# Seven block products in place of eight in layer 0, and sums begun in PSUM by ACT, in a four-layer graph kernel

## Chip, core and metric

One NeuronCore of a Trainium2 chip runs the whole kernel. The metric is device time in microseconds, as the median of several runs. Everything is float32.

The engines named below are PE (matrix products, results in PSUM), ACT and DVE (elementwise work, both read and write PSUM), POOL (elementwise work on SBUF alone) and SP, which issues all the DMAs here. PSUM has eight banks of 128 x 512 float32; a bank is one tile `ps`.

## What is computed

The input `x` is 64 graphs x 256 nodes x 128 features; one 256 x 256 adjacency matrix `adj` serves all. Four layers follow one another, each of the form x = layernorm(x + f(x)):

```python
def step(h, _):                                   # layer 0: five of these steps
    m_in = jnp.einsum('nm,bmd->bnd', in_matrix, h)
    m_out = jnp.einsum('nm,bmd->bnd', out_matrix, h)   # both matrices are adj
    av = jnp.concatenate([m_in, m_out], axis=-1)
    u3 = h @ u3_w.T + u3_b
    z = jax.nn.sigmoid(av @ w3_w.T + w3_b + u3)
    r = jax.nn.sigmoid(av @ w4_w.T + w4_b + u3)
    hv = jnp.tanh(av @ w5_w.T + w5_b + (r * h @ u5_w.T + u5_b))
    h = (1.0 - z) * h + z * hv
...
# layer 1: A = softmax of edge values; M = identity
out = einsum('ij,bjg->big', A * M, x @ W[0]) + einsum('ij,bjg->big', A * (1 - M), x @ W[1]) + bias
# layer 2: attention over adj (softmax of leaky scores, times adj), layernorm, relu -> h_gat
h_gin = (1.0 + eps) * h_gat + einsum('mn,bnh->bmh', A_final, h_gat)
z = relu(layernorm(h_gin @ W1 + b1));  f = relu(z @ W2 + b2 + h_gat)
# layer 3: x, adj x, adj^2 x, adj^3 x, each times a weight, for two copies of adj; their sum
```

## The kernel before

**Tiling.** Two graphs make a pair; there are 32 pairs. A pair's state is one 128 x 512 tile: four blocks of 128 nodes x 128 features (graph b, node half j, block 2b + j). What a layer needs the other way round (features on partitions) is the state turned.

**Message product.** `spread(i, right)` (L499) computes the product with a 256 x 256 matrix, and leaves it turned in one PSUM bank: for each graph b the two node halves are the stationary operands and two rows of blocks of `right`, 256 columns wide, are streamed. That is four products of 256 columns, or eight block products of 128 x 128 x 128. A float32 product is two matmul instructions, each with a weight load of its own. `to_sbuf` (L463) and `evacuate` (L208) copy the bank to SBUF, by ACT or DVE. `spread` is called five times in layer 0 with `aT`, once in layer 1 (`offT`), once in layer 2 (`ginT`) and once in layer 3 (`aT`).

**Layer 0** (L592) runs five steps. Each is a spread, five products of 512 columns (L599, L600, L607, L614, L615), three Tanh by ACT (L603, L609, L617), four elementwise operations of DVE (L605, L619, L620, L622), and a turn of the new state.

**Turning** (`turn`, L471) goes by DMA for most pairs: DVE transposes 32 x 32 blocks (L486), one DMA stores the tile to DRAM (L488), four more load it back (L494). For the last `BY_DMA[site]` pairs of a site PE transposes instead (L480), and ACT or DVE copies the result out.

**The other layers.** `products` (L630) multiplies the four blocks by one or two 128 x 128 weights, 128 columns at a time (L636). Its result in PSUM gets a bias or a residual added by DVE on the way out: L652 in layer 1, L718 and L725 in layer 2. `scale_stats` (L547) takes the mean square by ACT or DVE, POOL raises it to the power -1/2 (L571), and `scale_tokens` (L574) multiplies by it, on ACT, DVE or POOL. Layer 1's diagonal part turns x1 and multiplies the turned tile by `drow` (L645), a row that PE makes from the diagonal at the start (L389). Layer 3 (L730) has the products with `vx`, `vq` (L743, L744) and with the square of adj (L751).

**Order.** Nothing is issued as it is written. Every operation goes to a `Schedule` (L82) with the engines it may run on, a duration for each, and what it reads and writes. `order` (L111) plans the program before it is built: at each turn it takes, of all operations whose inputs are planned, the one that can start first (for operations with several possible engines, the one that ends first), ties by a due time (`DUE` per pair, `LAST_DUE` for the last `LAST` pairs, `HOLD` per layer). `MARGIN` stretches the durations of all engines but PE, `LAG` and `SEEN` are added before another engine sees a result. `PORT` (L40) keeps a POOL operation and a `DVE+` operation (two inputs from SBUF) apart in the plan. Tiles come from the counts in `CLASSES` (L36): 34 working tiles `A`, 15 states `X`, 8 banks `PS`. Each engine then runs its own list strictly in the planned order, each instruction waiting on semaphores for what it needs.

Of the kernel before, what the change touches and what calls it, by code (L numbers as in the profile page):

```python
# [17 lines left out]
BY_DMA = {"h": 1, "y": 1, "x1": 2, "x2": 1, "w": 0, "z": 1, "x3": 1}  # L18

WARM = 4  # L20

# [19 lines left out]


DUE, LAST_DUE, LAST = 15.0, 7.0, 6

MARGIN, LAG = 1.1, 0.3

HOLD = (0.0, 0.0, 0.0, 110.0)
# [7 lines left out]
class Value:  # L55
# [6 lines left out]

    def at(self, *shape):

        n = 1
        for s in shape:
            n *= s
        t = self.ap[:, :n]
        if len(shape) < 2:
            return t  # L70
        names = "abcd"[:len(shape)]
        return t.rearrange(f"p ({' '.join(names)}) -> p {' '.join(names)}", **dict(zip(names[1:], shape[1:])))

# [8 lines left out]
class Schedule:  # L82
# [6 lines left out]
    def add(self, ways, r=(), w=(), dma=None):  # L89

        op = Op(self.pair, ways, list(r), list(w), len(self.ops), dma)
        for v in op.reads:
            op.before.update(dict.fromkeys(v.writers))
        for v in op.writes:
            op.before.update(dict.fromkeys(v.readers))
        for v in op.reads:
            v.readers.append(op)
        for v in op.writes:  # L100
            v.writers.append(op)
        op.before.pop(op, None)
        op.layer = self.layer
        self.ops.append(op)
        return op
# [5 lines left out]
    def order(self, tiles):  # L111
        for op in self.ops:
            op.waits = len(op.before)
            for b in op.before:
                b.then.append(op)
            for v in dict.fromkeys([*op.reads, *op.writes]):
                v.left += 1
        for op in reversed(self.ops):
            us = min(w[1] for w in op.ways) + op.seen
            op.rest = us + max((x.rest for x in op.then if x.pair == op.pair), default=0.0)  # L120
        free = {cls: [(0.0, t) for t in ts] for cls, ts in tiles.items()}
        engines = dict.fromkeys([*SEEN, "PORT"], 0.0)
        ready = [op for op in self.ops if not op.waits]
        out, moved = [], 0.0
        while ready:
            best = None
            for op in ready:
                held = 0.0
                for v in op.writes:
                    if v.cls and v.ap is None:  # L130
                        held = max(held, min((t for t, _ in free[v.cls]), default=1e9))
                if held == 1e9:
                    continue
                for engine, us, fn in op.ways:
                    us = us if engine == "PE" else us * MARGIN
                    start = max(op.ready, held, *(engines[e] for e in USES.get(engine, (engine,))))
                    late = self.due(op.pair) - op.rest + HOLD[op.layer] if op.pair >= 0 else -1e4
                    key = (start + (us if len(op.ways) > 1 else 0.0), late, op.number)
                    if best is None or key < best[0]:
                        best = key, start, op, engine, us, fn  # L140
            if best is None:
                raise RuntimeError("no operation can start: too few tiles")
            _, start, op, engine, us, fn = best
            ready.remove(op)
            for v in op.writes:
                if v.cls and v.ap is None:
                    slot = min(free[v.cls], key=lambda s: s[0])
                    free[v.cls].remove(slot)
                    v.ap = slot[1]
            end = start + us  # L150
            engines.update(dict.fromkeys(USES.get(engine, (engine,)), end))
            if op.dma:
                wait, move, seen = op.dma
                moved = max(moved, end + wait) + move * MARGIN
                op.seen = moved + seen - end + LAG
            out.append((start, op.number, op, fn))
            for v in dict.fromkeys([*op.reads, *op.writes]):
                v.left -= 1
                v.end = max(v.end, end + op.seen)
                if not v.left and v.cls:  # L160
                    free[v.cls].append((v.end, v.ap))
            for x in op.then:
                x.waits -= 1
                same = engine != "SP" and x.ways[0][0].rstrip("+") == engine.rstrip("+")
                x.ready = max(x.ready, end + (0.0 if same else op.seen))
                if not x.waits:
                    ready.append(x)

            for v in dict.fromkeys([*op.reads, *op.writes]):
                op.__dict__.setdefault("tiles", {})[v] = v.ap  # L170
        assert len(out) == len(self.ops), "operations that wait for one another"
        self.span = max(engines.values())
        return [(op, fn) for _, _, op, fn in sorted(out, key=lambda x: x[:2])]
# [3 lines left out]
def kernel(ctx: ExitStack, tc: tile.TileContext, x, xT, adj, adjT, mats, cols, rows, out):  # L177
# [206 lines left out]

    drow, offT = fixed([N], "drow"), fixed([2, N], "offT")

    def diagonal():
        for it in range(2):
            nc.tensor.matmul(t4.at(2, P)[:, it, :], ones.ap[:, :P], dg.ap[:, it, :], start=True, stop=True)  # L389
    pe(mm(256), diagonal, [ones, dg], [t4])  # L390
    dve(0.4, lambda: nc.vector.tensor_copy(drow.ap, t4.at(N)), [t4], [drow])
# [53 lines left out]

    centre(vx, lambda: vx.ap, 2)
    centre(vq, lambda: vq.ap, 2)


# [49 lines left out]
    def spread(i, right):  # L499

        t = Value("PS", name="ps")
        for b in range(2):
            def fn(b=b):
                for j in range(2):
                    nc.tensor.matmul(t.at(2, N)[:, b, :], tokens(i)[:, 2 * b + j, :], right.ap[:, j, :],  # L505
                                     start=(j == 0), stop=(j == 1))
            pe(mm(512), fn, [i, right], [t])
        return t

# [82 lines left out]
    def layer0(x0, hT):  # L592
        h = x0
        for s in range(STEPS):
            mT = to_sbuf(spread(h, aT), "mT")
            t = Value("PS", name="ps")
# [14 lines left out]
            t = Value("PS", name="ps")  # L611
# [18 lines left out]
    def products(lefts, rights, name="ps"):  # L630

        t = Value("PS", name=name)
        for c in range(4):
            def fn(c=c):
                for k, (i, w) in enumerate(zip(lefts, rights)):
                    nc.tensor.matmul(tokens(t)[:, c, :], tokens(i)[:, c, :], w(), start=(k == 0), stop=(k == len(lefts) - 1))  # L636
            pe(mm(128 * len(lefts)), fn, [*lefts, W1], [t])
        return t

    def layer1(x1):  # L640
        qT = to_sbuf(spread(x1, offT), "qT")
        xb, dd = Value("A", name="xb"), lambda: drow.ap[:, None, :].to_broadcast([P, 2, N])
        if by_dma("x1"):
            dT = turn(x1, "dT", "x1")
            dve_or_pool(lambda e: e.tensor_mul(dT.at(2, N), dT.at(2, N), dd()), [drow, dT], [dT])  # L645
        else:
            t, dT = transposes(x1), Value("A", name="dT")
            dve(TT, lambda: nc.vector.tensor_mul(dT.at(2, N), t.at(2, N), dd()), [t, drow], [dT])
        dve_or_pool(lambda e: e.tensor_add(tokens(xb), tokens(x1), row("l1_bias", 4)), [x1, rbc], [xb])
        o = products([qT, dT], [lambda: mat("l1w1"), lambda: mat("l1w0")])  # L650
        y = Value("A", name="y")
        dve(TT, lambda: nc.vector.tensor_add(tokens(y), tokens(o), tokens(xb)), [o, xb], [y])  # L652
        scale_norm(y, x1)

    def layer2(x2):
# [20 lines left out]
        nm, nm2, den, d2 = (lambda k=k: s.at(32)[:, 4 * k:4 * k + 4] for k in range(4))  # L676
# [6 lines left out]
        def largest():  # L683
            nc.vector.tensor_add(nm(), nm(), hs()[:, :, D])
            nc.vector.tensor_scalar(nm2(), nm(), -1.0, None, op0=ALU.mult)
            nc.vector.scalar_tensor_tensor(nm(), nm(), -0.2, nm2(), op0=ALU.mult, op1=ALU.min)
        dve2(0.5, largest, [s, h], [s])
# [12 lines left out]
        t = Value("PS", name="ps")  # L700
        for b in range(2):
            def fn(b=b, t=t):
                for it in range(2):
                    for jt in range(2):
                        nc.tensor.matmul(tokens(t)[:, 2 * b + it, :], wT.at(8, P)[:, 4 * b + 2 * it + jt, :],  # L705
                                         hs()[:, 2 * b + jt, :D], start=(jt == 0), stop=(jt == 1))
            pe(mm(512), fn, [wT, h], [t])
# [8 lines left out]
        t = products([gT], [lambda: mat("w1")])  # L716
        z = Value("A", name="z")
        dve(TT, lambda t=t: nc.vector.tensor_add(tokens(z), tokens(t), row("b1", 4)), [t, rbc], [z])  # L718
        scale_norm(z, z)
# [3 lines left out]
        t = products([zT], [lambda: mat("w2")])  # L723
        y = Value("A", name="y")
        dve(TT, lambda t=t: nc.vector.tensor_add(tokens(y), tokens(t), tokens(hb)), [t, hb], [y])  # L725
        dve2(TT, lambda: nc.vector.scalar_tensor_tensor(y.at(512), y.at(512), 0.0, x2.at(512), op0=ALU.max, op1=ALU.add),
            [y, x2], [y])
        layer_norm(y, x2)

    def layer3(x3, p):  # L730
# [5 lines left out]
        for i in range(2):  # L736
            t = Value("PS", name="ps")
# [80 lines left out]
```

## Time and profile before

| | |
|---|---|
| median of 7 runs | 1520.1 us (1519.96 to 1520.8) |
| the profiled execution's own time | 1520.64 us |
| its span, first to last instruction | 1518.9 us |
| granted PE clock | 0.999 |
| DMA, mean busy share of 16 engines | 69.3% (queue q1), 215.34 MB |

The span is what the profile divides. The page gives busy times by engine, the same in 40 slices, the DMA queues, the chain of work that ended last, and groups of instructions by line of the code. A busy PE is a modelled figure, since its instructions overlap: an instruction of 512 columns is shown as 592 ns, while the next starts some 430 ns later. Prices of products are therefore taken from the distance between starts, which is what the chain gives. A DVE instruction too is shown with a tail that the next one overlaps.

Waits that the trace names most (us in total): ACT L603 on PE L600, 162.0; ACT L617 on PE L615, 160.6; ACT L210 on PE L505, 126.7; DVE L605 on ACT L603, 76.9; DVE L619 on ACT L617, 65.9. PE is in the list only with 0.33 us on a DMA, and with "issue" gaps of its weight loads, which lie under products that run.

### The profile page before, as it was taken

What the parts mean: (1) busy time and instruction counts of PE and PEld (TensorE: products, weight loads), DVE (VectorE), ACT (ScalarE), POOL (GpSimd) and SP (SyncE); (2) the same over time, 40 slices, a digit from 0 to 9 for tenths busy, and PEclk for the clock granted to TensorE, in tenths of its full rate; (3) what the DMA queues carried; (4) which work ended last, traced back from release to release, by engine and by line L of the source; (5) the groups of instructions that cost most, each with busy time, mean ns of one, the idle gap of its engine ahead of it and who ended that gap; (6) DMA issues with size and microseconds to landing.
All of it is one profiled execution on the core that took longest, in us unless ns stands there. A gap on an engine that the chain in (4) does not pass through costs nothing.

```text
span 1518.9 us, 22720 instructions
## 1 busy us (share of the span) xinstructions
PE 1511.0 (99%) x6300; PEld 1052.4 (69%) x6300; DVE 1184.0 (78%) x2774; ACT 901.4 (59%) x2497; POOL 362.7 (24%) x461
## 2 busy tenths in 40 slices
PE   9999999999999999999999999999999999999998
PEld 6555566666666766777677767666776676779987
DVE  6567878888898879888878778778787877887763
ACT  3444445566667767767656665656565556676752
POOL 0000001122323413332222303112331122224542
PEclk9999999999999999999999999999999999999999
DMA  8354557677688697877968777748677767575562
GB/s 237 73 111 97 118 115 149 140 145 161 146 173 158 150 187 149 175 150 170 171 130 174 153 153 160 160 98 164 140 148 152 147 133 144 103 144 118 119 131 64
DMA packets 949454, 216.79 MB, mean 143 GB/s; under 512 B 728144, under 2 KB 944848, under 8 KB 949328
## 3 DMA queue, kind: packets, MB, share of 16 engines
q1 hardware_dynamic: 949328, 215.34, 69.3%
q8 instruction: 51, 0.84, 0.2%
q14 instruction: 75, 0.61, 0.1%
HBM read 117.12 MB, written 98.11 MB: 142 GB/s over the span
## 4 chain that ended last, share of the span: by engine, by line
PE 99%; DMA 1%; SPq 0%; issue 0%; DVE 0%; POOLq 0%; ACT 0%; ACTq 0%; POOL 0%; DVEq 0%
PE ps L505 29%; PE ps L614 9%; PE ps L615 9%; PE ps L607 9%; PE ps L599 9%; PE ps L600 9%; PE ps L636 8%; PE ps L705 4%; PE ps L751 4%; PE ps L743 4%; PE ps L744 4%; PE ps L664 2%; DMA x<-x_in 0%; SPq L494 0%; PE ps L270 0%; PE ps L480 0%
## 5 line engine op out<-in xcount | busy, mean ns | idle before, releaser
L210 ACT COPY a<-ps 128x512 f32<-128x512 f32 (+1 forms) x295 | 160.3, 545 | 187.3 <-PE ps L505 126.7
L505 PE MATMUL ps<-aT,a 128*128 128x256 f32 x1024 | 242.7, 379 | 0.3 <-DMA a<-e 0.3
L505 PEld LDWEIGHTS ps<-aT,a 128*128 128x128 f32 x1024 | 193.4, 190 | 69.1 <-issue 45.4
L603 ACT ACTIVATE a<-ps,bzrh 128x512 f32<-128x512 f32 x160 | 109.9, 687 | 167.4 <-PE ps L600 162.0
L617 ACT ACTIVATE a<-ps,bzrh 128x512 f32<-128x512 f32 x160 | 109.8, 687 | 164.1 <-PE ps L615 160.6
L614 PE MATMUL ps<-a,w 128*128 128x512 f32 x320 | 163.5, 592 | 0.0
L600 PE MATMUL ps<-a,w 128*128 128x512 f32 x320 | 163.4, 592 | 0.0
L615 PE MATMUL ps<-a,u5h 128*128 128x512 f32 x320 | 163.4, 592 | 0.0
L607 PE MATMUL ps<-a,w 128*128 128x512 f32 x320 | 162.9, 592 | 0.0
L636 PEld LDWEIGHTS ps<-W,a 128*128 128x128 f32 x1024 | 128.9, 192 | 21.6 <-issue 18.9
L486 DVE STREAM_TRANSPOSE a<-a 128x512 f32<-128x512 f32 x186 | 131.0, 706 | 11.4 <-ACT a L582 4.2
L571 POOL TENSOR_TENSOR s<-s,neg_half 128x4 f32<-128x4 f32 x128 | 137.1, 1072 | 10.1
L605 DVE SCALAR_TENSOR_TENSOR a<-a,a 128x512 f32<-128x512 f32 x128 | 88.6, 692 | 63.0 <-ACT a L603 60.1
L609 ACT ACTIVATE a<-ps,bzrh 128x512 f32<-128x512 f32 x160 | 109.8, 686 | 45.6 <-PE ps L607 43.7
L619 DVE TENSOR_TENSOR a<-a,a 128x512 f32<-128x512 f32 x128 | 90.0, 703 | 54.8 <-ACT a L617 54.6
L636 PE MATMUL ps<-W,a 128*128 128x128 f32 x1024 | 131.3, 275 | 0.0
L599 PE MATMUL ps<-a,W 128*128 128x512 f32 x256 | 130.8, 593 | 0.0
L524 POOL TENSOR_SCALAR s<-s 128x4 f32<-128x4 f32 x64 | 21.4, 334 | 453.3 <-DVE s L521 444.6
L620 DVE SCALAR_TENSOR_TENSOR a<-a,a 128x512 f32<-128x512 f32 x160 | 117.3, 733 | 12.2 <-ACT a L609 7.1
L568 POOL TENSOR_SCALAR s<-s 128x4 f32<-128x4 f32 x96 | 29.0, 302 | 392.6 <-ACT a L563 304.8
L505 PE MATMUL ps<-aT,x 128*128 128x256 f32 x512 | 122.3, 382 | 0.1
L600 PEld LDWEIGHTS ps<-a,w 128*128 128x128 f32 x320 | 60.8, 190 | 76.5 <-issue 72.5
(181 smaller groups left out, 2731.5 us busy)
## 6 DMA issues: line engine op xcount, KB each, us to landing
e<-a SPq DMA_DIRECT2D x278, 256.0 KB
a<-e SPq DMA_DIRECT2D x1112, 64.0 KB
e<-b SPq DMA_DIRECT2D x32, 512.0 KB
b<-e SPq DMA_DIRECT2D x128, 128.0 KB
x<-x_in SPq DMA_DIRECT2D x32, 256.0 KB
t<-xT_in SPq DMA_DIRECT2D x32, 256.0 KB
a<-d SPq DMA_DIRECT2D x32, 256.0 KB
y_out<-a SPq DMA_DIRECT2D x32, 256.0 KB
```

Of the source, the lines that this page charges most:

```text
L210: S.add([("ACT", us[0], lambda: nc.scalar.copy(o(), i())), ("DVE", us[1], lambda: nc.vector.tensor_copy(o(), i()))], r, w)
L486: dve(n / 512 * 0.55 + 0.09, lambda: nc.vector.transpose(st.at(n), i.at(n)), [i], [st])
L505: nc.tensor.matmul(t.at(2, N)[:, b, :], tokens(i)[:, 2 * b + j, :], right.ap[:, j, :], start=(j == 0), stop=(j == 1))
L571: pool(1.02, lambda: nc.gpsimd.tensor_tensor(rs(), rs(), neg_half.ap, op=ALU.pow), [s, neg_half], [s])
L599: nc.tensor.matmul(t.at(512), mat("u3"), hT.at(512), start=True, stop=False)
L600: nc.tensor.matmul(t.at(512), w4.ap, mT.at(512), start=False, stop=True)
L603: act(0.59, lambda t=t, r=r: nc.scalar.activation(r.at(512), t.at(512), AF.Tanh, bias=bzrh.ap[:, 1:2], scale=0.5), [t, bzrh], [r])
L607: pe(mm(512), lambda t=t, mT=mT: nc.tensor.matmul(t.at(512), w3.ap, mT.at(512), start=False, stop=True, skip_group_check=True), [w3, mT, t ...
L614: nc.tensor.matmul(t.at(512), w5.ap, mT.at(512), start=True, stop=False)
L615: nc.tensor.matmul(t.at(512), u5h.ap, r.at(512), start=False, stop=True)
L620: dve2(TT, lambda hv=hv, z=z: nc.vector.scalar_tensor_tensor(hv.at(512), z.at(512), 1.0, hv.at(512), op0=ALU.add, op1=ALU.mult), [hv, z], ...
L636: nc.tensor.matmul(tokens(t)[:, c, :], tokens(i)[:, c, :], w(), start=(k == 0), stop=(k == len(lefts) - 1))
```

## The change

**Layer 0's message product.** A new `spread7` takes the place of `spread` and its copy, in all five steps (`FAST`) of pairs 0 to 28 (`FIRST`, `FINAL`). It treats the four blocks of the state as a 2 x 2 block matrix (graph by node half) and multiplies it by the 2 x 2 blocks of `aT` with seven block products (Winograd's form of Strassen's scheme). Four sums of state blocks are formed first, by DVE or POOL; four sums of blocks of `aT` (`aTt`) are made once at the start. The products go to the four quarters of one bank, some of them added to what an earlier product left there; between them DVE adds and ACT or DVE copies read single quarters of the same bank.

**Sums begun in PSUM.** `seed` copies a residual or a bias from SBUF into a bank (ACT, or DVE), and `products` adds to it, so the separate DVE additions L652, L718 and L725 go. `scale_norm` then reads the bank itself, and so does the last sum of layer 2 (L726). The planner gives a seed only a bank whose last value was written by products over its whole width.

**Smaller parts.** Layer 1 scales x1 by the diagonal as a column before the turn, in place of after it; `drow` and its products (L389) go. Three small DVE operations for the softmax become two (L684 to L686). `BY_DMA` changes: layer 0's last pair now turns by DMA, and one more pair each at `y`, `x1`, `x2`, `x3` and three at `w` turn on PE. The planner's constants change, and a dependent operation on the same engine is now planned 0.12 us later (`AGAIN`).

```diff
-BY_DMA = {"h": 1, "y": 1, "x1": 2, "x2": 1, "w": 0, "z": 1, "x3": 1}
+BY_DMA = {"h": 0, "y": 2, "x1": 3, "x2": 2, "w": 3, "z": 1, "x3": 2}
+FAST = (0, 1, 2, 3, 4)
+FIRST, FINAL = 0, 3
+AGAIN = {"DVE": 0.12, "POOL": 0.12}
+SPARE = {"DVE": 0.0, "DVE+": 0.0, "POOL": 0.0}
-DUE, LAST_DUE, LAST = 15.0, 7.0, 6
-MARGIN, LAG = 1.1, 0.3
-HOLD = (0.0, 0.0, 0.0, 110.0)
+DUE, LAST_DUE, LAST = 20.0, 9.0, 8
+MARGIN, LAG = 1.03, 0.8
+HOLD = (0.0, -20.0, 0.0, 80.0)
...
-                        held = max(held, min((t for t, _ in free[v.cls]), default=1e9))
+                        held = max(held, min((t for t, a in free[v.cls] if full.get(id(a)) or not v.seeded), default=1e9))
...
-                x.ready = max(x.ready, end + (0.0 if same else op.seen))
+                x.ready = max(x.ready, end + (AGAIN.get(engine.rstrip("+"), 0.0) if same else op.seen))
...
-    def diagonal():
-        for it in range(2):
-            nc.tensor.matmul(t4.at(2, P)[:, it, :], ones.ap[:, :P], dg.ap[:, it, :], start=True, stop=True)
-    pe(mm(256), diagonal, [ones, dg], [t4])
-    dve(0.4, lambda: nc.vector.tensor_copy(drow.ap, t4.at(N)), [t4], [drow])
+    dcol, offT = fixed([2], "dcol"), fixed([2, N], "offT")
+    dve(0.3, lambda: nc.vector.tensor_reduce(dcol.ap, dg.ap, AX.X, ALU.add), [dg], [dcol])
...
+    aTt = fixed([4, P], "aTt")
+    blk_a = lambda j, i: aT.ap[:, j, i * P:(i + 1) * P]
+    for k, (p_, q_) in enumerate(((lambda: blk_a(0, 1), lambda: blk_a(0, 0)), (lambda: blk_a(1, 1), lambda: aTt.ap[:, 0, :]),
+                                  (lambda: blk_a(1, 1), lambda: blk_a(0, 1)), (lambda: blk_a(1, 0), lambda: aTt.ap[:, 1, :]))):
+        dve(0.25, lambda k=k, p_=p_, q_=q_: nc.vector.tensor_sub(aTt.ap[:, k, :], p_(), q_()), [aT, aTt], [aTt])
...
+    def seed(us, o, i, r):
+        t = Value("PS", name="ps")
+        t.seeded = True
+        evacuate(lambda: o(t), i, r, [t], us)
+        return t
...
+    def spread7(h, right, terms):
+        sv, t, o = Value("A", name="sums"), bank(), Value("A", name="mT")
+        p1, p2, p3, p4 = (Part(sv) for _ in range(4))
+        X, Y, Z, V = (Part(t) for _ in range(4))
+        o1, o2, o3 = (Part(o) for _ in range(3))
+        blk = lambda v, k, n=1: v.at(512)[:, k * P:(k + n) * P]
+        H = lambda b, j: lambda: blk(h, 2 * b + j)
+        B = lambda j, i: lambda: right.ap[:, j, i * P:(i + 1) * P]
+        T = lambda k: lambda: terms.ap[:, k, :]
+        s1, s2, s3, s4 = (lambda k=k: blk(sv, k) for k in range(4))
+        def add(o, x, y, op, r, w):
+            fn = lambda e: e.tensor_tensor(o(), x(), y(), op=op)
+            S.add([("DVE+", 0.2, lambda: fn(nc.vector)), ("POOL", 0.42, lambda: fn(nc.gpsimd))], r, w)
+        def product(k, left, rt, r, w, start=False):
+            pe(mm(128), lambda: nc.tensor.matmul(blk(t, k), left(), rt(), start=start, stop=True, skip_group_check=True),
+               [*r, right, terms], w)
+        def plus(to, k, other, r, w, n=1):
+            dve(0.065 + 0.135 * n, lambda: nc.vector.tensor_add(to(), t.at(4, P)[:, k:k + n, :], other()), r, w)
+        def copy(to, k, r, w):
+            S.add([("ACT", 0.18, lambda: nc.scalar.copy(to(), blk(t, k))),
+                   ("DVE", 0.2, lambda: nc.vector.tensor_copy(to(), blk(t, k)))], r, w)
+        product(0, H(0, 0), B(0, 0), [h], [X, Y, Z, V], start=True)
+        copy(lambda: blk(o, 3), 0, [X], [o3])
+        add(s1, H(1, 0), H(1, 1), ALU.add, [h], [p1])
+        add(s2, s1, H(0, 0), ALU.subtract, [h, p1], [p2])
+        add(s3, H(0, 0), H(1, 0), ALU.subtract, [h], [p3])
+        add(s4, H(0, 1), s2, ALU.subtract, [h, p2], [p4])
+        product(0, H(0, 1), B(1, 0), [h, X], [X])
+        copy(lambda: blk(o, 0), 0, [X], [o])
+        product(1, s2, T(1), [p2, Y], [Y])
+        plus(lambda: blk(sv, 1), 1, lambda: blk(o, 3), [Y, o3], [p2])
+        product(2, s1, T(0), [p1, V], [V])
+        product(3, s3, T(2), [p3, Z], [Z])
+        plus(lambda: blk(sv, 0), 2, lambda: blk(sv, 1), [V, p2], [p1])
+        product(2, s4, B(1, 1), [p4, V], [V])
+        plus(lambda: blk(o, 3), 3, lambda: blk(sv, 0), [Z, p1, o3], [o])
+        product(3, H(1, 1), T(3), [h, Z], [Z])
+        plus(lambda: o.at(4, P)[:, 1:3, :], 2, lambda: blk(sv, 1)[:, None, :].to_broadcast([P, 2, P]), [V, Z, p2], [o], 2)
+        return o
...
-            mT = to_sbuf(spread(h, aT), "mT")
+            mT = spread7(h, aT, aTt) if s in FAST and FIRST <= S.pair < n_pairs - FINAL else to_sbuf(spread(h, aT), "mT")
...
-        o = products([qT, dT], [lambda: mat("l1w1"), lambda: mat("l1w0")])
-        y = Value("A", name="y")
-        dve(TT, lambda: nc.vector.tensor_add(tokens(y), tokens(o), tokens(xb)), [o, xb], [y])
-        scale_norm(y, x1)
+        t = seed((0.49, 0.61), tokens, lambda: tokens(xb), [xb, qT, dT])
+        scale_norm(products([qT, dT], [lambda: mat("l1w1"), lambda: mat("l1w0")], t), x1)
...
-        t = products([gT], [lambda: mat("w1")])
-        z = Value("A", name="z")
-        dve(TT, lambda t=t: nc.vector.tensor_add(tokens(z), tokens(t), row("b1", 4)), [t, rbc], [z])
-        scale_norm(z, z)
+        t, z = seed((0.49, 0.61), tokens, lambda: row("b1", 4), [rbc, gT]), Value("A", name="z")
+        scale_norm(products([gT], [lambda: mat("w1")], t), z)
...
-        t = products([zT], [lambda: mat("w2")])
-        y = Value("A", name="y")
-        dve(TT, lambda t=t: nc.vector.tensor_add(tokens(y), tokens(t), tokens(hb)), [t, hb], [y])
-        dve2(TT, lambda: nc.vector.scalar_tensor_tensor(y.at(512), y.at(512), 0.0, x2.at(512), op0=ALU.max, op1=ALU.add),
-            [y, x2], [y])
+        t, y = seed((0.49, 0.61), tokens, lambda: tokens(hb), [hb, zT]), Value("A", name="y")
+        products([zT], [lambda: mat("w2")], t)
+        dve(TT, lambda t=t: nc.vector.scalar_tensor_tensor(y.at(512), t.at(512), 0.0, x2.at(512), op0=ALU.max, op1=ALU.add),
+            [t, x2], [y])
```

## The prediction

> **What bounds the kernel now.** I read the page's busy times first, then the chain of waits, then the chain in order of time for the price of each product, then stages of the run for the slack of the other engines.
>
> ```profile
> PE 1511.0 (99%) x6300; PEld 1052.4 (69%) x6300; DVE 1184.0 (78%) x2774; ACT 901.4 (59%) x2497; POOL 362.7 (24%) x461
> PE 99%; DMA 1%; SPq 0%; issue 0%; DVE 0%; POOLq 0%; ACT 0%; ACTq 0%; POOL 0%; DVEq 0%
> ```
>
> The busy share alone would prove little, but the chain that ended last is PE too: each product is released by the product before it, not by DVE, ACT or a transfer. PE runs from 1.20 to 1512.6 us nearly without a gap, then 6.3 us of statistics and the store remain. So a product's price is on the path, and all other work is free while it arrives in time.
>
> ```profile
> 20.07 0.22 PE ps L314 x2
> 43.01 3.45 PE ps L505 x16
> 46.47 0.86 PE ps L599 x2
> 502.00 3.57 PE ps L636 x32
> 1471.94 0.44 PE ps L480 x4
> ```
>
> Columns: start, us, what, instructions. Two instructions make one product. L505 gives 3.45/8 = 0.431 us for 256 columns, so a whole spread is 1.725. L599 gives 0.86 for 512. L636 gives 3.57/16 = 0.223 for 128 columns, 3.5% dearer per column. L314 streams a single column and still takes 0.22: that is the price of the two weight loads, so 128 columns are where the load and the stream meet. Four transposes on PE cost 0.44.
>
> ```profile
> 400.00:600.00 200.00, 199.67 (x840) 134.97 (x839) 173.89 (x386) 140.54 (x400) 63.58 (x70) 1.00 0.83 164
> 1450.00:1480.00 30.00, 30.00 (x162) 27.00 (x161) 18.09 (x59) 15.92 (x63) 11.77 (x19) 1.00 0.52 106
> ```
>
> Columns: length; busy PE, weight loads, DVE, ACT, POOL; clock, DMA share, GB/s. In the fullest stage DVE is 87% busy, and PE still misses only 0.33 us of 200. That is the headroom that matters.
>
> **The products.** 29 pairs x 5 steps = 145 spreads become seven products each: 7 x 0.223 = 1.562 in place of 1.725, 0.163 saved, **-23.6 us**. If a lone 128-column product between wider ones hides its loads under them, it costs half of a 256-wide product, 0.2157, and the saving is 145 x 0.215 = 31.2; I keep that as the other end and take the row of like shape.
>
> **The turns moved.** The last pair's four turns of layer 0 leave PE: -4 x 0.44. One each comes to PE at y, x1, x2, x3 (4 x 0.44) and three double ones at w (6 x 0.44): net **+2.6 us**. On SP's queue the moved turns exchange 4 sets of one store and four loads for 4 others and three larger ones: fewer issues at the very end, and no new one ahead of older work. The diagonal's two products go: **-0.4**.
>
> **The work that feeds the products.** Per fast step DVE gets three 128-wide additions from PSUM and one 256-wide, DVE or POOL four 128-wide sums, ACT or DVE two 128-wide copies; one 512-wide copy goes.
>
> ```profile
> L276 DVE TENSOR_TENSOR w<-W 128x128 f32<-128x128 f32 x3 | 0.8, 290 | 3.4 <-DMA W<-mats_in 3.3
> L584 DVE TENSOR_TENSOR a<-ps,s 128x256 f32<-128x256 f32 x38 | 14.8, 412 | 10.9 <-POOL s L571 10.3 <-ACT a L210 0.5
> L652 DVE TENSOR_TENSOR a<-ps,a 128x512 f32<-128x512 f32 x32 | 21.6, 676 | 6.7 <-PE ps L636 6.5
> L718 DVE TENSOR_TENSOR a<-ps,rbc 128x512 f32<-128x512 f32 x32 | 21.7, 680 | 12.4 <-PE ps L636 12.4
> L725 DVE TENSOR_TENSOR a<-ps,a 128x512 f32<-128x512 f32 x32 | 21.7, 678 | 8.2 <-PE ps L636 8.0
> L210 ACT COPY a<-ps 128x512 f32<-128x512 f32 x242 | 140.6, 583 | 142.2 <-PE ps L505 126.7 <-PE ps L480 6.5 <-DMA a<-e 4.5
> L563 ACT ACTIVATE a<-ps 128x128 f32<-128x128 f32 x196 | 51.8, 276 | 25.1 <-PE ps L751 16.6 <-PE ps L705 8.3
> L649 POOL TENSOR_TENSOR a<-x,rbc 128x512 f32<-128x512 f32 x13 | 17.9, 1378 | 62.0 <-ACT x L540 41.9 <-PE ps L614 12.2 <-DVE x L535 7.9
> ```
>
> A DVE addition of 128 columns is 0.29 alone; two of them in a row took 0.49 in the timeline at 8.84, so 0.20 each in a stream. With 0.38 for the 256-wide one, the additions from PSUM are 3 x 0.20 + 0.38 = 0.98 per step, 142 us. The sums on DVE are 4 x 0.20 x 145 = 116; on POOL a 128-wide sum lies between its 4-wide row (0.25, L570) and 1.38 at 512, by a line some 0.53, 307 us in all. DVE loses L652, L718, L725 (65 us) and one small softmax operation (6): 1184 - 71 + 142 = 1255 with the sums on POOL, 1371 with them on DVE, of about 1500: **84 to 91%**. POOL ends between 24 and 45%. ACT: 96 seeds at 0.58 add 56, 290 copies at 0.28 add 81, 145 copies of 512 go (-85): 901 becomes 953, 64%. I cost all of this at nothing, since PE stands in front of it; what covers it is the deferred products of layer 3 (L743, L744, L751) and the steps of other pairs. Without that cover a step's hand-overs would show, which is the second rival. The scaling of x1 changes place with the turn and is priced the same.
>
> A seed makes four `products` wait for one copy by ACT. What stands behind it on PE is the next pair's work, in strict order; the planner adds 0.8 us (`LAG`) before PE counts on another engine's result, where it added 0.3. Bounds per seed: 0, or one ACT copy plus the hand-over, 0.58 + 0.25 (PE L505 ended its modelled chain piece at 4.98 + 4.66, ACT's second copy began 0.04 later, so 0.25 is generous), 96 x 0.83 = 80 us at worst; I take 0, by the 0.33 us in the stage above, where copies by ACT already stand between products.
>
> [...]
>
> **Start and stalls.** PE begins its third spread only at 18.07 us: until then two pairs are at work, and PE has little else to do. A fast step's chain is add, add, product, three additions, product, last addition: about 0.29 x 2 + 0.45 + 3 x 0.35 + 0.45 + 0.45 = 3.0 us (0.45 being a product with the hand-over to the next engine or the wide addition, 0.35 a short addition on top of the one it waits for), against 1.73 + 0.59 for spread and copy. One to two us later per step for the first pairs, over some two steps: 0 to 6, I take **+3**. Elsewhere 0 to 8, I take **+1**.
>
> **Sum.** 1520.6 - 23.6 + 2.6 - 0.4 + 3 + 1 = 1503.2 for the profiled execution; it lies 0.5 above the median, so 1502.7, rounded to **1502**. The low end is the cheaper product without stalls: 1520.1 - 31.2 + 2.2 = 1491.
>
> **Rivals.** (1) **DVE becomes the bound**, slower than before. For it: 87% already in the fullest stage, where 21 more fast steps (200/47 pairs) would add 21 x 0.98 to 21 x 1.78 = 21 to 37 us and take away 9, so 186 to 202 of 197. Against it: POOL had 68% of that stage free, ACT takes the seeds, and DVE is half idle in the first 80 and last 70 us. Price: all sums and seeds on DVE (1371 + 96 x 0.68) and 0.10 lost at four dependent additions per step (58) make 1494, plus some 45 us at the two ends that it can't use: 1539. It decides once DVE's demand passes about 1455, that is 1500 less those 45.
>
> (2) **Hand-overs show on PE.** Seven products with sums between them, in strict order: if one step in six has an uncovered hand-over of 0.6 us (0.25 + 0.29 + semaphore), 14 us go, and the time is 1516. For it: ACT already waits 162 us on L600, so plans are tight there. Against it: PE's own waits are 0.33 us in all before.
>
> (3) **The loads hide**, and the change gives more than the row of L636 says: 1494. For it: the streamed work next to a product is often 512 wide. Against it: L636 in runs of four costs the same 0.223 as in runs of sixteen.
>
> **How the numbers follow.** Forecast 1496 to 1511: 0.57. (3), below 1496: 0.08. (2), 1511 to 1523: 0.15, half of it still faster. (1): 0.20. A difference of 0.2% (3 us) is what runs of this kernel can tell from none. Faster 0.57 + 0.08 + 0.07 = 0.72, same 0.08, slower 0.20. The range 1490 to 1524 leaves out (1) and little at the low end.
>
> **What would show it.** Right: PE still 99% of the chain; the 145 fast steps in the chain as pairs of instructions 0.22 apart; L505 down from 29% of the chain to about 12%, the new product lines together near 15%; DVE between 84 and 91%; no group of PE waiting on DVE above a few us. Wrong: PE idle before the new products, released by DVE or POOL (rivals 1 and 2), or PE's clock falling in such gaps; a price per product other than 0.223; additions of DVE much over 0.29 because POOL's sums hold them up. If DVE stands in the chain with more than 5%, the forecast is wrong.

## The result, and the profile after

The changed kernel takes **1524.1 us** (median of 13 runs, 1522.8 to 1526.6) against 1520.1 (31 runs, 1519.0 to 1521.3): a ratio of 1.0027, 95% interval 1.002 to 1.0034. It is 4 us slower, where 1502 was forecast, just past the end of the range (1490 to 1524). The profiled execution took 1524.7 us with a span of 1522.9, at a granted clock of 0.998.

The page's busy times and its chain of waits, after:

```profile
PE 1502.2 (99%) x7190; PEld 1063.2 (70%) x7190; DVE 1294.0 (85%) x3443; ACT 937.0 (62%) x2805; POOL 558.7 (37%) x784
PE 90%; DVE 4%; DMA 2%; SPq 2%; issue 1%; ACT 0%; POOLq 0%; ACTq 0%; DVEq 0%; POOL 0%
```

PE is still shown as 99% busy, but it no longer is the whole chain: a tenth of it now runs through DVE, transfers and their queue. The loads on DVE, ACT and POOL are near those of the forecast (84 to 91%, 953 us, 24 to 45%).

The same two stages as before:

```profile
400.00:600.00 200.00, 197.58 (x973) 139.30 (x973) 177.64 (x483) 136.97 (x429) 85.79 (x116) 1.00 0.82 160
1450.00:1480.00 30.00, 30.00 (x170) 27.21 (x169) 19.20 (x60) 19.78 (x72) 10.57 (x16) 1.00 0.41 89
```

PE misses 2.42 us of the full stage, where it missed 0.33. The last stage, which has none of the new products, is full as before.

The new products in the chain in order of time:

```profile
109.19 2.68 PE ps L562 x24
```

Twelve products in 2.68 us are 0.223 each, the price that was forecast. So the products cost what they should, and the time went into gaps between them. The waits of their line (its own view: us, times) and two rows of the list of waits (us, times, longest):

```profile
  issue: 81.0, 323
  DVE a L566: 18.9, 40
  ACT a L569: 13.1, 26
  POOL a L558: 2.2, 9
```

```profile
ACT a L569 <- PE ps L562: 84.6, 93, 5.6
ACT a L569 <- DVE a L566: 40.9, 48, 2.9
```

L562 is `product`, L566 `plus` (DVE adds a quarter of the bank to a tile), L569 `copy` (ACT copies quarter 0 out), L558 the sums of state blocks. The view adds the idle time of PE and of its weight loads, so its figures aren't time lost by themselves ("issue" lies under running products, as before). But two things in them need a reason: **products wait for ACT's copy**, and **ACT's copy waits 41 us for DVE's addition**. ACT only reads quarter 0 of the bank, which no `plus` touches. In the built program the first fast step shows it plainly: the second copy, of quarter 0, waits for the addition that reads quarter 1.

One such moment in the timeline (start, us, engine, line; in brackets the idle time and what ended it):

```profile
522.58 0.39 PE L562 MATMUL ps<-aTt,a 128*128 128x128 f32 x2
...
523.06 0.27 ACT L569 COPY a<-ps 128x128 f32<-128x128 f32 x1 [1.15 <-PE ps L562]
...
523.47 0.46 PE L562 MATMUL ps<-aTt,a 128*128 128x128 f32 x2 [0.50 <-ACT a L569]
```

The second product has `aTt` as its right operand. Such products write quarters 1, 2 and 3; the copy reads quarter 0. Nothing that the product needs comes from the copy, and PE stands 0.5 us for it.

**How much PE stands.** The gaps have to be separated from the pipelining of PE. I take the distance between the starts of consecutive PE instructions; its median is 429 ns for 512 columns, 216 for 256 and 112 for 128, as for a single column. Number times median is PE's work; what a distance exceeds its median by, where that is over 40 ns, is counted as standing.

| | time | PE's work | standing | of it before the new products |
|---|---|---|---|---|
| before | 1520.1 | 1508.2 | 4.2 | |
| after | 1524.1 | 1487.2 | 29.7 | 24.4, in 101 places |

Work fell by 21.0 us, standing rose by 25.5: together +4.5, of which the times show +4.0. What has to be explained above all is 24.4 us of standing in front of 1015 products. The 101 places are 46 products that begin late (19.2 us, in 38 of the 145 fast steps) and 55 second instructions of a product, some 0.1 us late each (5.2 us), most of them right behind such a late beginning.

### The profile page after: what moved, and what is told of

It is laid out like the page before. It is cut to its first block, busy times and chain, and to the rows that moved or that the text cites. A ratio compares the mean times of both kernels' runs of the same rounds, so it can differ in the third digit from the quotient of the medians.

```text
span 1522.9 us, 26241 instructions
## 1 busy us (share of the span) xinstructions
PE 1502.2 (99%) x7190; PEld 1063.2 (70%) x7190; DVE 1294.0 (85%) x3443; ACT 937.0 (62%) x2805; POOL 558.7 (37%) x784
## 4 chain that ended last, share of the span: by engine, by line
PE 90%; DVE 4%; DMA 2%; SPq 2%; issue 1%; ACT 0%; POOLq 0%; ACTq 0%; DVEq 0%; POOL 0%
PE ps L562 13%; PE ps L539 12%; PE ps L679 8%; PE ps L680 8%; PE ps L694 8%; PE ps L695 8%; PE ps L687 8%; PE ps L716 7%; PE ps L786 4%; PE ps L830 4%; PE ps L822 3%; PE ps L823 3%; PE ps L746 2%; SPq L528 2%; DVE a L566 1%
## 5 line engine op out<-in xcount | busy, mean ns | idle before, releaser
L566 DVE TENSOR_TENSOR a<-ps,a 128x128 f32<-128x128 f32 (+1 forms) x580 | 175.3, 315 | 92.9 <-PE ps L562 76.5
L562 PEld LDWEIGHTS ps<-aTt,a 128*128 128x128 f32 x1102 | 160.8, 192 | 60.5 <-issue 42.0
L562 PE MATMUL ps<-aTt,a 128*128 128x128 f32 x1102 | 180.1, 277 | 4.9 <-ACT a L569 3.7
L558 POOL TENSOR_TENSOR a<-a 128x128 f32<-128x128 f32 x138 | 82.3, 610 | 236.0 <-DMA a<-e 111.9
L562 PEld LDWEIGHTS ps<-aT,a 128*128 128x128 f32 x754 | 118.2, 191 | 52.3 <-issue 34.8
L569 ACT COPY a<-ps 128x128 f32<-128x128 f32 x265 | 66.4, 266 | 130.4 <-PE ps L562 84.6
L562 PE MATMUL ps<-aT,a 128*128 128x128 f32 x754 | 136.7, 278 | 5.7 <-DVE a L566 3.8
L231 ACT COPY a<-ps 128x512 f32<-128x512 f32 (+1 forms) x162 | 82.7, 514 | 73.8 <-PE ps L539 36.9
L643 ACT ACTIVATE a<-ps 128x128 f32<-128x128 f32 x428 | 112.8, 283 | 22.9 <-PE ps L716 9.5
L648 POOL TENSOR_SCALAR s<-s 128x4 f32<-128x4 f32 x96 | 28.9, 301 | 250.5 <-ACT a L643 219.8
```

Of the source, the lines that this page charges most:

```text
L562: pe(mm(128), lambda: nc.tensor.matmul(blk(t, k), left(), rt(), start=start, stop=True, skip_group_check=True), [*r, right, terms], w)
L566: dve(0.065 + 0.135 * n, lambda: nc.vector.tensor_add(to(), t.at(4, P)[:, k:k + n, :], other()), r, w)
L643: nc.scalar.activation(tokens(junk)[:, c, :], v.at(len(tiles), D)[:, k, :], AF.Square, scale=D ** -0.5, accum_out=mv()[:, c, 1:2])
```

## The experiments

Two theories were put against each other. **A**: DVE and POOL are too full to feed the products in time (rival 1). **B**: the plan takes the quarters of a bank as independent (`Part` X, Y, Z, V), but in the built program the semaphores keep accesses of different engines to one bank in order, whichever quarter they touch; so the plan counts on overlaps that don't happen. Times are medians; each ratio is to the kernel before on the same chip.

**Sums of state blocks left out.**

```diff
-            S.add([("DVE+", 0.2, lambda: fn(nc.vector)), ("POOL", 0.42, lambda: fn(nc.gpsimd))], r, w)
+            S.add([("DVE+", 0.2, lambda: None), ("POOL", 0.42, lambda: None)], r, w)
...
-        product(1, s2, T(1), [p2, Y], [Y])
+        product(1, H(0, 0), T(1), [p2, Y], [Y])
```

> The four sums of state blocks in each fast step are left out, and the products take state blocks in their place, so layer 0 computes something else. The order of everything else, on every engine, is that of the changed kernel. The sums are 269 us of instructions on DVE and POOL together. In the changed kernel PE stands for 29.7 us between products (distance between starts above the usual one for the size), 24.4 of it in front of the new products. Theory A (DVE and POOL are too full, so sums and what stands behind them come late): most of the 24.4 goes, PE stands for under 12 us in all, and the time falls to some 1503 to 1508 us. Theory B (accesses to one PSUM bank are kept apart by semaphores, so that a product waits for a read of another quarter of its bank, which the plan does not know): the bank waits are all still there; PE still stands for 18 us or more, and the time is 1512 us or more.

Measured: 1518.1 us (0.9989, 0.998 to 0.9998). POOL lost 177 us of work and DVE 84, and only 6.0 us came back; 19.2 us of standing before the new products stayed. A is at most this part.

**Additions and copies read SBUF in place of the bank**, same sizes, same number, same plan.

```diff
-            dve(0.065 + 0.135 * n, lambda: nc.vector.tensor_add(to(), t.at(4, P)[:, k:k + n, :], other()), r, w)
+            dve(0.065 + 0.135 * n, lambda: nc.vector.tensor_add(to(), terms.ap[:, k:k + n, :], other()), r, w)
...
-            S.add([("ACT", 0.18, lambda: nc.scalar.copy(to(), blk(t, k))),
+            S.add([("ACT", 0.18, lambda: nc.scalar.copy(to(), terms.ap[:, k, :])),
```

> The copies and additions between the seven products read the constant tile of sums of adjacency blocks in SBUF instead of the bank, so layer 0 computes something else. Their number, engines, sizes and order are those of the changed kernel, and so is the order of the products. Theory B (bank waits): nothing reads the bank while products write it, so PE's 24.4 us in front of the new products fall below 8, and the time to some 1502 to 1508 us. Theory A (DVE and POOL too full): DVE has as much to do as before, and its additions now share the port with POOL, so the time stays within 1520 to 1530 us.

Measured: 1508.9 us (0.9928, 0.9913 to 0.9944). Standing before the new products fell from 24.4 to 4.9 us, while DVE became fuller; the time lies 0.9 us above B's range. Its busy times and chain, and the waits of L562:

```profile
PE 1492.7 (99%) x7190; PEld 1061.4 (70%) x7190; DVE 1317.5 (87%) x3443; ACT 935.7 (62%) x2805; POOL 577.3 (38%) x784
PE 87%; DVE 6%; SPq 2%; DMA 2%; issue 1%; ACT 0%; POOL 0%; POOLq 0%; DVEq 0%; ACTq 0%
```

```profile
  issue: 85.9, 358
  DMA x<-x_in: 3.9, 3
  POOL a L558: 2.8, 9
  DVE a L558: 2.0, 6
...
  DVE a L566: 0.7, 3
```

The waits on L569 are gone and those on L566 fell from 18.9 to 0.7, those on the sums (L558) stayed small. A would have wanted the opposite: more DVE, more waiting. In the changed kernel's trace a sum on DVE (L558, both inputs in SBUF) took 282 ns on average where no addition or other TENSOR_TENSOR of POOL ran beside it (207 sums), and 542 ns, at most 1378, where one ran for over half of it (46 sums); an addition that reads the bank (L566, 128 wide) took 283 ns in both cases. That agrees with a DVE that is fuller here, 1317.5 us for 1294.0. The chain line warns the reader: DVE's share of it is larger here (6%) than in the changed kernel (4%), in a run 15 us faster. The chain follows who released whom, also where that cost no time.

This run takes away true waits with the false ones, since a product that adds to a quarter must wait for the addition that reads it. So the next run takes one kind alone.

**Only the copies read SBUF.** The edit is the second half of the one above.

> Only the two copies per fast step (nearly all on ACT) read the constant tile in SBUF in place of the bank; the additions of DVE read the bank as in the changed kernel. So two quarters of a step's message are not computed as they should be. Order, sizes and engines stay. Theory B: about a third to a half of the standing in front of the new products is put down to ACT's copies of the first quarter, so 8 to 12 us go and the time is 1511 to 1517 us. Theory A: ACT is 62% busy and not the trouble; nothing goes, 1521 to 1526 us.

Measured: 1514.4 us (0.9965, 0.9953 to 0.9977), standing 20.1 in all, 13.6 before the new products. 9.6 us hang on 290 short copies, nearly all by ACT, whose only direct tie to a product is within quarter 0 (the second product waits for the first copy). The first copy also feeds the first addition, and this run frees that path too.

The waits written into the built program, laid beside the trace of the changed kernel, tell true waits from false ones. Of the 46 late products, 37 (15.8 us) waited last for a read of another quarter of their bank, 23 times by DVE and 14 times by ACT. For 34 of these 37 all that the product needs from other engines, its inputs and its own quarter, had been ready for longer than PE then stood. The waits for ACT's copy in the product's own quarter come to 0.4 us. In the run in which nothing reads the bank, no product waits last for another quarter.

**The rest of the change without the seven products.**

```diff
-FAST = (0, 1, 2, 3, 4)
+FAST = ()
```

with the planner's constants of before, and `LAST_DUE` 8, `LAST` 5.

> The change without the seven products (no step is fast), with the planner's constants and the turns by DMA of the kernel before, but for two due times of the last pairs. What is left is the sums begun in PSUM, the scaling of x1 before its turn, and two small softmax operations in place of three. Product work is that of the kernel before. My prediction's step (seeds cost nothing, DVE loses some 70 us): PE still bound, 1518.5 to 1521.5 us, DVE about 1110 us busy. Rival (a seed in front of products shows on PE): 96 seeds at 0.3 to 0.8 us each would give 1545 us or more; half of that, 1530.

Measured: 1520.4 us against 1519.7 on that chip (1.0006, 0.9997 to 1.0015), standing 3.8.

```profile
PE 1509.7 (99%) x6296; PEld 1051.0 (69%) x6296; DVE 1118.8 (74%) x2733; ACT 917.9 (60%) x2476; POOL 365.4 (24%) x468
```

DVE lost 65 us of additions, ACT gained 17, and nothing moved: seeds cost nothing and gain nothing here. The loss comes with the seven products, or with the planner's constants and turns that were changed beside them and that this run puts back.

**Using the bank by turns.** If B holds, an order that lets PE and the readers have the bank one after the other, and tells the plan so, should win. The products become two operations of four and three, each taking the whole bank; between them one operation of three additions.

```diff
+        def first():
+            mul(0, H(0, 0), B(0, 0), start=True)
+            mul(3, s3, T(2))
+            mul(2, s1, T(0))
+            mul(1, s2, T(1))
+        pe(mm(512) + 0.03, first, [h, right, terms, p1, p2, p3], [t])
+        copy(lambda: blk(o, 3), 0, [t], [o, t])
...
+        dve(0.84, middle, [t, o, p1, p2], [o, t, p1, p2])
...
+        pe(mm(384) + 0.03, second, [h, right, terms, p4, t], [t])
```

A first try had `LAG` 0.3, `DUE` 25 and `HOLD` (0, 0, 0, 130); beside it ran the changed kernel with these same constants, the same turns with `LAG` 0.5, and the changed kernel's order of products with a plan that takes the whole bank (`X = Y = Z = V = t`, reads count as writes).

> The same seven products, sums and additions in another order, which uses the bank in turns: one operation of four products (P1, P3, P4, P5) into the four quarters, then all that reads them, then one operation of the three products that add (P2, P6, P7), then the last reads; and the plan is told that the whole bank is taken by each. Planner's constants: LAG 0.3, DUE 25, HOLD (0, 0, 0, 130). Theory B (bank waits that the plan doesn't know): the 24.4 us of standing in front of the new products fall below 8 and the time to some 1500 to 1508 us. Theory A (DVE and POOL too full): the work is the same, DVE as full, 1520 us or more.

> The changed kernel with nothing but the planner's constants of the run in rounds (LAG 0.3, DUE 25, HOLD (0, 0, 0, 130)): the control for it. Theory B: with less slack before a result counts, the unknown bank waits come through in full: slower than the changed kernel, 1525 to 1560 us. Rival C (only the constants matter, the order in the bank does not): as fast as the run in rounds, within 3 us of it.

> The run in rounds with more slack: LAG 0.5, DUE 20, HOLD (0, -20, 0, 90). Theory B: fewer late hand-overs on PE than with 0.3, but the plan itself leaves some 5 us more of PE open: 1502 to 1510 us. Rival C: the constants decide, and this one lies between the changed kernel (LAG 0.8) and the run with 0.3.

> The changed kernel's own order of the seven products and their reads, one by one, but the plan is told that each access takes the whole bank (LAG 0.3, DUE 25, HOLD (0, -20, 0, 110)). Theory B: the waits are now in the plan, so that other work stands there; what stays is the plan's own open time, some 17 us more than in the run in rounds, since each step now has six turns of the bank in place of two: 1508 to 1520 us. Theory A: as the changed kernel or slower, 1524 us and more.

| | time | ratio, 95% | standing | before the new products |
|---|---|---|---|---|
| turns, `LAG` 0.3 | 1545.6 | 1.0154, 1.014 to 1.0168 | 52.2 | 12.4 |
| changed kernel, `LAG` 0.3 | 1544.9 | 1.0155, 1.0141 to 1.0169 | 46.9 | 38.7 |
| turns, `LAG` 0.5 | 1526.8 | 1.004, 1.0027 to 1.0054 | 30.6 | 8.4 |
| own order, plan told, `LAG` 0.3 | 1547.1 | 1.0173, 1.0159 to 1.0187 | 51.8 | 28.2 |

B's forecast was missed in three of the four; only the control came out as it said. By their times alone they read as the rivals forecast: the first two lie within 1 us of each other (C), the third lies between the changed kernel and the run with 0.3 (C), and the fourth is above 1524 us (A). Turns did what B says where it says it, 38.7 to 12.4 us at the same constants, but the standing came back elsewhere: in front of layer 2's attention products (L797, 11.4 us), of the products that add to seeds (L727, 7.1), of the old spread (L539, 5.2) and of layer 0's products with `u5h` (L706, 4.8).

In the fourth run the false waits went too: products that waited last for another quarter fell from 60 (22.0 us) in the control to 13 (4.0 us), with `HOLD` changed as well. Other waits took their place, transfers first:

```profile
PE ps L562 <- DMA a<-e: 6.4, 8, 1.8
```

PE's waits in the turns with `LAG` 0.5:

```profile
PE ps L797 <- DMA b<-e: 4.6, 6, 1.7
PE ps L757 <- DMA a<-e: 3.3, 2, 2.0
```

L797 and L757 are both layer 2's products (the attention, and the projection ahead of it), and what they wait for are turned tiles loaded from DRAM. My reading is that with `LAG` 0.3 the plan counts on results sooner than they come, so that engines and transfers drift late, and PE, in strict order, stands for whichever is late. That is not shown by itself: no run changes `LAG` alone, and the kernel before, with `LAG` 0.3 and `MARGIN` 1.1, stands 4.2 us in all. What is shown is that the changed kernel with 0.3, and `DUE` and `HOLD` of this set, is 21 us slower. So the planner's constants matter beside the bank, and B had to be tried under better ones.

**Turns with `LAG` 0.6, and two banks.** The second kernel leaves products and reads in smaller turns, but uses two banks for a step, so that PE can write one while DVE reads the other. With each comes the changed kernel under its very constants.

```diff
-DUE, LAST_DUE, LAST = 20.0, 9.0, 8
-MARGIN, LAG = 1.03, 0.8
-HOLD = (0.0, -20.0, 0.0, 80.0)
+DUE, LAST_DUE, LAST = 23.0, 12.0, 7
+MARGIN, LAG = 1.05, 0.6
+HOLD = (0.0, 0.0, 5.0, 105.0)
...
+        pe(mm(256) + 0.015, first, [h, right, terms, p2], [t])
+        pe(mm(256) + 0.015, other, [h, right, terms, p1, p3], [t2])
```

(The constants are those of the turns, the last two lines of the kernel with two banks, which has `DUE` 20, `LAST_DUE` 3, `LAST` 6 and `HOLD` (0, 0, 0, 115). `BY_DMA` differs too, by one or two pairs a site.)

> The same seven products, sums and additions, but in two banks: P1, P2, P3 in two quarters of one, P4 to P7 in two quarters of another, so that DVE and ACT read one bank while PE writes the other; the plan takes each bank whole, so the waits that the semaphores make are in it. Planner's constants: LAG 0.6, MARGIN 1.05, DUE 20, LAST_DUE 3, LAST 6, HOLD (0, 0, 0, 115), and two entries of the turns on PE. Theory B: standing in front of the new products below 8 us (24.4 in the changed kernel), time 1505 to 1514 us, faster than the kernel before. Theory A (DVE and POOL too full): the work is the same, 1520 us or more.

> The order in rounds in one bank again, now with LAG 0.6 and MARGIN 1.05 (DUE 23, LAST_DUE 12, LAST 7, HOLD (0, 0, 5, 105)). The first two runs of it lost PE to late transfers and late copies at LAG 0.3 and 0.5, not to the bank. Theory B with enough slack: 1512 to 1520 us. If the order in rounds is itself too slow for PE (a step's chain in one bank is longest here), it stays above 1522.

> The control for the run with two banks: the changed kernel's own seven products in one bank, the plan not told of the bank, with the planner's constants of the run with two banks. Theory B: the unknown waits stay, standing in front of the new products 15 us or more, and the time is 4 us or more above the run with two banks: 1512 to 1522 us. Rival C (the constants alone decide): within 2 us of the run with two banks.

> The control of e10: the changed kernel's own order of products and reads, the quarters of a bank taken as independent by the plan, with the planner's constants of e10 and nothing else changed. Bank waits (B): the constants give at most a few us, so 1515 to 1527, 8 to 18 us above e10's 1508.0, with 15 to 28 us of PE standing in front of the new products, against e10's 4.5. Slack alone: if e10's gain came from its constants and not from using the bank by turns, 1505 to 1512 with under 8 us standing there.

| | time | ratio, 95% | PE's work | standing | before the new products |
|---|---|---|---|---|---|
| turns, one bank | 1508.0 | 0.9916, 0.9903 to 0.993 | 1486.7 | 13.2 | 4.5 |
| changed kernel, its constants | 1527.8 | 1.0053, 1.0036 to 1.007 | 1486.7 | 32.6 | 20.7 |
| two banks | 1509.6 | 0.992, 0.9906 to 0.9933 | 1484.9 | 17.7 | 11.7 |
| changed kernel, its constants | 1520.6 | 0.9997, 0.9987 to 1.0007 | 1484.9 | 27.6 | 18.4 |

These two pairs settle that the use of the bank matters apart from the constants. Same products, same sums and additions, same constants; only the use of the bank differs, and the times differ by 19.8 and 11.0 us, the standing by 19.4 and 9.9. In the first control 31 products (15.3 us) again waited last for another quarter. Order, grouping and plan change together within each pair, so the pairs don't say what each of the three is worth. The turns did better than expected (1512 to 1520), the expectation of under 8 us of standing for two banks missed (11.7), and the last control came out 0.8 us above its range. The turns' busy times and chain:

```profile
PE 1491.5 (99%) x7186; PEld 1061.0 (70%) x7186; DVE 1308.2 (87%) x3403; ACT 948.3 (63%) x2796; POOL 600.1 (40%) x839
PE 96%; DVE 2%; DMA 1%; SPq 1%; issue 0%; ACT 0%; POOLq 0%; ACTq 0%; POOL 0%; DVEq 0%
```

Against the changed kernel DVE and POOL are both busier, and PE is back at 96% of the chain. PE's own waits before the new products (L575 here) in the turns:

```profile
PE ps L575 <- DVE a L588: 2.6, 2, 2.2
...
PE ps L575 <- DVE a L556: 0.2, 1, 0.2
```

and in the changed kernel with the same constants:

```profile
PE ps L562 <- DVE a L566: 5.1, 9, 1.2
...
PE ps L562 <- ACT a L569: 3.5, 6, 1.4
...
PE ps L562 <- DVE a L570: 1.2, 3, 0.5
```

These rows leave out what its weight loads and its sequencer wait, so they are smaller than the standing; but 18 short waits on the bank's readers have become two, on an addition. Both variants leave nothing out, and beat both kernels: each by 0.8% of the time before.

## Why the forecast missed

**What failed.** The step is "Elsewhere 0 to 8, I take +1", with its ground, "I cost all of this at nothing, since PE stands in front of it". The runs put 24.4 us of standing in front of the new products. Of these the first 100 us hold 6.1 (all standing there was 8.5 after, 3.2 before), the upper end of the term of +3 with its bounds of 0 to 6. The other 18.3 were to be in the +1. With standing as forecast (4.2 + 3 + 1 = 8.2 in place of 29.7) the time would have been 1524.1 - 21.5 = 1502.6.

**Why.** I looked for lack of capacity: busy shares, and the 0.33 us that PE missed in the fullest stage. That stage had no products which alternate with reads of the same bank: a spread filled its bank, then one copy emptied it. A busy share says nothing of a chain of three engines that take turns at one bank, add, copy, product, each in its strict order, and each planned as if the others' quarters were elsewhere. The program built from this kernel has waits that keep accesses of different engines to one bank in order, and the 40.9 us that ACT's copies of quarter 0 wait for DVE's additions to other quarters agree with it. The change meant DVE to read one quarter while PE writes another; in the built program PE waits, and 37 late products (15.8 us) waited last for a read of another quarter, 23 times by DVE and 14 times by ACT. I didn't ask which waits the built program would put between engines at one bank, and the planner's `Part` doesn't know them.

**Point by point.** PE's work: forecast -23.6 + 2.6 - 0.4 = -21.4 us, measured -21.0. Right. A product's price, 0.223: right. The low end, a lone short product between wider ones that costs less, is not what the chain in order of time shows:

```profile
589.93 3.45 PE ps L539 x16
593.39 0.22 PE ps L562 x2
593.61 0.43 PE ps L822 x2
```

One new product stands between 256-wide ones and takes its 0.22. Seeds at nothing: right, by the run without the seven products. Loads of DVE, POOL and ACT: within the forecast's bounds. POOL's 128-wide sum, 0.53 by a line, was this:

```profile
L558 POOL TENSOR_TENSOR a<-a 128x128 f32<-128x128 f32 x138 | 82.3, 610 | 236.0 <-DMA a<-e 111.9 <-DVE a L702 39.2 <-PE ps L695 15.5
L558 DVE TENSOR_TENSOR a<-a,a 128x128 f32<-128x128 f32 x124 | 38.7, 318 | 0.9
L566 DVE TENSOR_TENSOR a<-ps,a 128x128 f32<-128x128 f32 x435 | 119.4, 283 | 81.4 <-PE ps L562 65.7 <-ACT a L569 5.4 <-ACT x L620 1.9
```

Up to 15% longer, and at no cost that the runs show beyond the 6.0 us of all sums together. The last row also shows DVE idle 81 us before its additions, 66 of them for PE: DVE isn't short of time there, it stands in a ring with PE.

**The rivals.** (1), DVE as the bound: no. At 87% the turns ran 1508.0. (2), hand-overs that show on PE, at 1516: the right place, with a size of 24.4 us in place of 14. It was priced as one step in six at 0.6 us; it was 38 steps of 145, about one in four, at 0.64 each. The price was near; what made them frequent were mostly waits that no product needed. (3), cheaper products: not seen.

**The signs to look for.** L562 at 13% and L539, the old spread, at 12% of the chain came near the forecast (15 and 12%), and PE waiting before the new products was named as what would show the forecast wrong. The sign with a number, "If DVE stands in the chain with more than 5%", was a bad one: DVE has 4% in the slow kernel and 6% in the run that reads SBUF, which is 15 us faster.

**What stays open.** How much of the changed kernel's 24.4 us would go with the waits on another quarter was read from the program's waits and the trace alone: 15.8 us at the spot, 19.4 with the late second instructions behind them, and lateness that they cause further on isn't counted. Taking only the false waits away, with the bank still shared, wasn't tried, so no run shows what that gives. What `LAG` a plan needs is open too: between 0.3 and 0.6 the turns gained 37.6 us, but `DUE`, `HOLD`, `MARGIN` and `BY_DMA` were changed with it.

## What to carry to other kernels

In this kernel 37 late products (15.8 us) waited last for another engine's read of a quarter of the bank that they didn't touch. So when a change makes engines alternate on one PSUM bank, look in the built program for such waits, and where it has them count the bank, not its columns, as the resource: ask of each access which engine's access to the same bank comes ahead of it, and plan it so. Telling the plan alone, in the old order, was not enough at the constants tried (1547.1 us). Many short reads between short products were dear here (24.4 us of standing) although DVE was 85% busy, ACT 62% and POOL 37%; a few larger turns, or a second bank, made the kernel 11 to 20 us faster at the same work. Before trusting "hidden", compare PE's work with its standing: the busy share and the chain's shares showed 99% and 90% where 2% of the time had gone.

## What the runs showed of the hardware beyond that

Sums begun in PSUM by ACT or DVE, with values other than zero, in banks that products had filled over their whole width, were added to as meant, 96 of them in the changed kernel; no run seeds another bank, so what happens there is not shown. In the run without the seven products 96 of them (85 by ACT) cost nothing that could be measured (1.0006, 0.9997 to 1.0015). In the profile of the changed kernel a 512-wide copy by ACT into a bank took 0.6 us:

```profile
L231 ACT COPY ps<-a 128x512 f32<-128x512 f32 x56 | 33.2, 595 | 0.8 <-DVE a L664 0.4 <-ACT a L689 0.4
```

PE's granted clock stayed between 0.994 and 1.0 in all runs, whatever the gaps between products.
